# Order of the row scatters, the routing steps and the residual steps on the queues of an attention and mixture-of-experts kernel

## The chip, the cores and the metric

The kernel runs on one core of one Trainium2 chip, in one launch. The metric is device time in microseconds. Three timed runs of the kernel before gave 1774.93, 1779.41 and 1780.96 us, so its time is the median, 1779.41 us. The profile comes from a separate execution in which the hardware profiler recorded every instruction.

A core has five engines with a queue of instructions each: PE (matrix products; its weight loads are listed apart as PEld), DVE (elementwise work on vectors), ACT (activations and copies), POOL (a general engine that here also issues the indirect transfers) and SP (which here only issues transfers). Each queue runs in order. Transfers are issued from POOL's and SP's queues and are carried out by 16 DMA engines.

## The reference, cut to what matters

The input is four sequences (batches) of 512 tokens of width 512. A first attention over the context adds to x; then comes a transformer block with causal attention and a mixture of experts. The change concerns the mixture and how its rows are laid out.

```python
x1 = x + xattn(layernorm(x), ctx)             # context attention, one per batch
hid = layernorm(x1)
h = rmsnorm(hid, ln1_w)                        # causal attention, 16 heads of 128
q, k, v = (heads(h @ w) for w in (wq, wk, wv))
ao = softmax(causal(q @ k.T / sqrt(128))) @ v
x2 = hid + merge(ao) @ wo
t = rmsnorm(x2, ln2_w).reshape(-1, 512)        # 2048 rows
probs = softmax(t @ gate_w.T)                  # 16 experts
topv, topi = top_k(probs, 6)
topv = topv / sum(topv)
cw = zeros(2048, 16).at[row, topi].add(topv)
routed = sum over e of cw[:, e] * ((silu(t @ eg_w[e].T) * (t @ eu_w[e].T)) @ ed_w[e].T)
shared = (silu(t @ sg_w.T) * (t @ su_w.T)) @ sd_w.T
out = x1 + x2 + routed + shared
```

An expert has 352 hidden features, the shared expert 704.

## The kernel before, in words

**Precision.** Operands of PE are split into a high and a low half-precision part, and each product is three matmuls (high by high, high by low, low by high). The helper that issues them gives nearly every matmul one of three source lines: L83, L86 and L87. The helper that splits a result (a copy on ACT and a subtraction on DVE or POOL) gives L73, L74, L77 and L78. So matmuls are told apart by the names of their tiles.

**Attention.** The outer loop runs over 64 heads `n`, in the order of `path`: batches 0 and 1 in turn by groups of two heads, then batches 2 and 3 likewise, so that a batch ends well before its partner's last groups. In each step PE does `queries` of head n (tile `qk`), every second step `values` (`v`), then, if a group is done, `project` (`wo`, four matmul groups over two banks, added into `x2` at L681), then `scores` of head n (`sc`, with the softmax on DVE and ACT and a transposing transfer of the result), and `attend` of head n-1 (`av`, evicted to `ao`). A generator, `step`, feeds in the context attention of the next batches (tiles `xm`, `hd`, `x_d`, `r`).

**Routing.** When the eighth group of a batch is projected, `route1` runs at once: sums of squares on ACT (`rsq`), then `rsqrt` (an addition on DVE and a power on POOL, L104, tile `rrs`), then for each of four row tiles the normalised rows `h2` (L494), their split into `h2p` and a transposing transfer by SP's queue into `h2T`. It also appends four entries to `rest`. `agenda` then calls `route2` at step n+2 and `route3` at step n+3. `route2` makes the gate's logits on PE (tile `lg`, L520, 64 small matmuls), the softmax, the top 6 and one-hot codes on DVE, and running sums over the experts and the product of probabilities on POOL (L559 to L562). `route3` counts rows per expert on PE (`rk`) and POOL, gives every row and choice a slot (L590, L591 and others), and appends 24 scatters to the list `scat`: four row tiles by six choices.

**Scatters, marks and residual steps.** A scatter (L463) is an indirect transfer from POOL's queue that writes the 128 rows of one `h2p` tile to their slots in `xs_d`, the experts' input in DRAM. Scatters are declared independent of each other, since their slots differ. `pace(src)` copies one element to `mark` on POOL (L455); it must wait for `src`, a result of the stage that runs then, and so holds what stands behind it on POOL's queue. `rest_step` loads a tile of the saved first residual (`x1t`, L506), adds `x2` (L509) and stores the sum to `r_d`. The list `scats` holds the marks and scatters made so far.

**Order of the queues.** The kernel is written in program order and a scheduler, which simulates the engines' times, decides the order in each queue. What must stay in order without data behind it is given by `after(ins, first)`, which adds a dependence for the order only. In the kernel before each mark and each scatter is placed behind the last entry of `scats`.

**Shared expert.** `gate_up` runs in six blocks `ic` for a batch (tiles `sg` and `su`, with SiLU at L710 and the product at L713 into `hs`); `shared_down` makes four row tiles `sy` and adds them into an accumulator `acc` at L735, which `residual(b)` loads from `r_d` over SP's queue (L689). Batch 0's shared expert runs at the end of the attention, then batch 1's (`up(1)`), with batch 3's `route2` and `route3` among its blocks, then batch 2's (`up(2)`). `drip(n, src)` is a mark and then up to n scatters. `rows_in` loads the first expert's rows from `xs_d`, transposed, into `xT`, again over SP's queue.

**Experts.** Sixteen experts follow in the order of their row counts (`g` and `u`, then `y`, stored to `y_d`), batch 3's shared expert comes last, and 96 indirect gathers (L1149) collect the results.

Of the kernel before, what the change touches and what calls it, by code (L numbers as in the profile page):

```python
# [10 lines left out]
F32 = mybir.dt.float32  # L11
# [3 lines left out]
ALU = mybir.AluOpType  # L15
AX = mybir.AxisListType

P = 128
B, S, D = 4, 512, 512
# [36 lines left out]
def xattn_moe_block_kernel(ctx: ExitStack, tc: tile.TileContext, x, xT, ctxT, wqkx, bqk, ln1, ln2,  # L56
# [36 lines left out]
    def after(ins, first):  # L93
        tc.add_manual_dep(ins.ins, first.ins.name,
                          mybir.DependencyInfo(mybir.DependencyClass.NoSync, mybir.DependencyReason.DATA),
                          reason="order on the queue")
# [4 lines left out]
    def rsqrt(o, v, eps):  # L101
        n = o.shape[1]
        nc.vector.tensor_scalar(o, v, eps, None, ALU.add)
        nc.gpsimd.tensor_tensor(o, o, mhalf[:, :n], ALU.pow)  # L104

    ident = const.tile([P, P], F32, name="ident")
    make_identity(nc, ident)
# [345 lines left out]

    def pace(src):
        ins = nc.gpsimd.tensor_copy(mark, src)  # L455
        if scats:
            after(ins, scats[-1])
        scats.append(ins)

    def scatter(n):  # L460
        while scat and n:
            tt, k = scat.pop(0)
            ins = nc.gpsimd.indirect_dma_start(  # L463
                out=xs_d, out_offset=bass.IndirectOffsetOnAxis(ap=slotu[:, tt, k:k + 1], axis=0),
                in_=h2ps[tt], in_offset=None)
            tc.declare_no_dep(ins.ins, group="scat", reason="the slots differ")
            tc.add_to_no_dep_group("scat", ins.ins)
            if scats:
                after(ins, scats[-1])
            scats.append(ins)  # L470
            n -= 1

# [8 lines left out]
    def route1(b, x2):  # L481
        ms = bsm.tile([P, NT], F32, name="rms")
        for t in range(NT):
            sq = xp.tile([P, D], F16, tag="h2", name="rsq", bufs=1)
            nc.scalar.activation(sq, x2[:, t, :], AF.Square, scale=1.0 / math.sqrt(D),
                                 accum_out=ms[:, t:t + 1])
        rr = bsm.tile([P, NT], F32, name="rrs")
        rsqrt(rr, ms, 1e-6)
        h2T[b] = hpool.tile([P, 2 * C, S], F16, tag="hT", name=f"h2T{b}")
        for t in range(NT):  # L490
            tt = b * NT + t
            tl = slice(t * P, (t + 1) * P)
            h2 = xp.tile([P, D], F32, tag="h2", name="h2", bufs=1)
            nc.vector.scalar_tensor_tensor(h2, x2[:, t, :], rr[:, t:t + 1], ln2b, ALU.mult, ALU.mult)  # L494
            h2p = h2ps[tt] = rp.tile([P, 2 * D], F16, tag="h2p", name="h2p", bufs=4)
            split1(h2p[:, :D], h2p[:, D:], h2, nc.vector if b == B - 1 else nc.gpsimd)
            zz["flip"] = flip(h2T[b][:, :, tl], h2p)
            rest.append((b, t, x2))
# [3 lines left out]
    def rest_step():  # L502
        if rest:
            b, t, x2 = rest.pop(0)
            x1t = xp.tile([P, D], F32, tag="x1t", name="x1t", bufs=1)
            ins = nc.gpsimd.dma_start(x1t, x1_d[b][:, t, :])  # L506
            if scats:
                after(ins, scats[-1])
            nc.gpsimd.tensor_tensor(x1t, x1t, x2[:, t, :], ALU.add)  # L509
            nc.gpsimd.dma_start(r_d[b][:, t, :], x1t)  # L510

# [53 lines left out]
    def route3(b):  # L565
        nonlocal macc
        oh, mm, cs, pr = zz[b]
        bs = slice(b * NT, (b + 1) * NT)
        rk = bank("s", f"rk{b}")
        for t in range(NT):  # L570
            o = rk[:, t * E:(t + 1) * E]
            nc.tensor.matmul(o, su, mm[:, t, :], start=True, stop=False)
            nc.tensor.matmul(o, onesm, macc, start=False, stop=True)
            m2 = const.tile([P, E], F16, tag="macc", name=f"macc{b}_{t}", bufs=3)
            nc.gpsimd.tensor_tensor(m2, macc, mm[:, t, :], ALU.add)
            macc = m2
        rb = rp.tile([P, NT, E], F32, name="rb", bufs=1)
        nc.vector.tensor_tensor(rb, rk[:, :NT * E].rearrange("p (t e) -> p t e", e=E),
                                ebase.unsqueeze(1).to_broadcast([P, NT, E]), ALU.add)
        o4 = oh.rearrange("p (t k) e -> p t k e", k=K)  # L580
        w4 = rp.tile([P, NT * K, E], F32, name="w4", bufs=1)
        for t in range(NT):
            nc.vector.tensor_tensor(o4[:, t], cs[:, t, :].unsqueeze(1).to_broadcast([P, K, E]),
                                    kp1.unsqueeze(2).to_broadcast([P, K, E]), ALU.is_equal)
        for dst, val in ((slot, rb), (cw, pr)):
            for t in range(NT):
                nc.gpsimd.tensor_tensor(w4[:, t * K:(t + 1) * K, :], o4[:, t],
                                        val[:, t, :].unsqueeze(1).to_broadcast([P, K, E]), ALU.mult)
            nc.vector.tensor_reduce(dst[:, bs, :].rearrange("p t k -> p (t k)"), w4, AX.X, ALU.add)
        nc.gpsimd.tensor_tensor(w4, oh, ioe.unsqueeze(1).to_broadcast([P, NT * K, E]), ALU.mult)  # L590
        nc.vector.tensor_reduce(tid[:, bs, :].rearrange("p t k -> p (t k)"), w4, AX.X, ALU.add)  # L591
        nc.vector.tensor_copy(slotu[:, bs, :], slot[:, bs, :])
        for t in range(NT):
            for k in range(K):
                scat.append((b * NT + t, k))
# [160 lines left out]
    for n in range(NH + LAG + 1):  # L756
        if n < NH:
            b, h = heads[n]
            if b not in opened:
                opened.add(b)  # L760
                step(b, 99)
                if b == B - 1:
                    shared_pool()
            parts = [queries(b, h)]
            if h % HG == 0:
                parts.append(values(b, h // HG))
            if n == 0:
                parts.reverse()
                for p in parts:
                    next(p)  # L770
            for p in parts:
                for _ in p:
                    pass
        m = n - LAG
        if n >= NH:
            for ic in range(3 * (n - NH), 3 * (n - NH) + 3):
                hs0 = next(early)
                if scat:
                    pace(hs0[ic // 3][0:1, ic % 3, 0, 0:1])
                    scatter(-(-len(scat) // (6 - ic)))  # L780
        if ready:
            b, g = ready.pop()
            project(b, g)
            left[b] -= 1
            if not left[b]:
                route1(b, x2s[b])
                agenda[n + 2] = agenda[n + 3] = b
                if stop == "B":
                    nc.sync.dma_start(out[b].rearrange("(t p) d -> p t d", p=P), x2s[b])
        if n < NH:  # L790
            scores(*heads[n])
        if 0 <= m < NH:
            b, h = heads[m]
            attend(b, h)
            if h % HG == HG - 1:
                ready.append((b, h // HG))
        if n in agenda and n < NH:
            b = agenda[n]
            if n + 1 in agenda:
                route2(b)  # L800
            else:
                route3(b)
        if m > 0 and (rest or scat):
            pace(aos[heads[m - 1][0], heads[m - 1][1] // HG][0:1, heads[m - 1][1] % HG, 1, 0:1])
        rest_step()
        if scat and n < NH:
            scatter(-(-len(scat) // (min(x for x in ends if x > n) - n + (4 if n > NH - 3 else 0))))
        shared_weights()
        if H // 2 <= n < H // 2 + E:
            pad_rows(n - H // 2)  # L810
        if n < 6:
            step(1, 2)
        else:
            for _, j in zip(range(2 - n % 2), bring):
                step(j)
# [12 lines left out]
    def up(b):  # L828
        return gate_up(b, lambda: st2.tile([P, 6 * S], F16, name="hs"), lambda: st2.tile([P, S], F32, name="sgt"))

    def drip(n, src):
        if scat:
            pace(src)
            scatter(n)

    ups = enumerate(up(1))
    _, hs = next(ups)
    route2(B - 1)
    for _, hs in zip(range(3), ups):
        hs = hs[1]  # L840
    route3(B - 1)

    cps = bank("s", "cnt")
# [22 lines left out]
            nc.vector.tensor_tensor(o, o, t, ALU.add)  # L866
        return o

    for _, hs in ups:
        pass  # L870
    drip(1, hs[1][0:1, 2, 0, 0:1])
    shared_down(1, hs, tick=lambda src: drip(2, src))
    residual(2)
    after(zz["exp"], zz["silu", 1, 1])
# [100 lines left out]
    seat(0)  # L975
    nxt = ranked_weights(0)
    for ic, hs in enumerate(up(2)):
        drip(3, hs[ic // 3][0:1, ic % 3, 0, 0:1])
        if ic == 4:
            rows_in(0, 0)  # L980
            rows_in(0, 1)
    shared_down(2, hs)
# [291 lines left out]
```

## Time and profile before

| | |
|---|---|
| median of three timed runs | 1779.41 us |
| the profiled execution's own time | 1810.57 us |
| its span, first to last instruction | 1808.8 us |
| mean granted clock of PE in it | 0.98 |
| DVE / ACT / POOL busy | 62% / 46% / 26% of the span |
| scatters L463 | 96, of 1009 ns mean, 96.8 us together |
| gathers L1149 | 96, of 1129 ns mean, 108.4 us together |
| transfers | 296.24 MB, mean 164 GB/s |

The profiled execution took 31.16 us more than the median of the timed runs, and 1.8 us of its time lie outside its span. Places in the text are given in microseconds from the start of the span. In a line of the timeline the first number is the start, the second the duration of the instruction or run of like instructions, then come engine, source line, operation, the tiles written and read, and in brackets the idle time of the engine just before it with what ended it. "issue" there means that the engine waited for nothing that the profile shows, "remote" for something that is not on this core or not known. In a list of waits the numbers are the total, how often, and the longest.

### The profile page before, as it was taken

What the parts mean: (1) busy time and instruction counts of PE and PEld (TensorE: products, weight loads), DVE (VectorE), ACT (ScalarE), POOL (GpSimd) and SP (SyncE); (2) the same over time, 40 slices, a digit from 0 to 9 for tenths busy, and PEclk for the clock granted to TensorE, in tenths of its full rate; (3) what the DMA queues carried; (4) which work ended last, traced back from release to release, by engine and by line L of the source; (5) the groups of instructions that cost most, each with busy time, mean ns of one, the idle gap of its engine ahead of it and who ended that gap; (6) DMA issues with size and microseconds to landing.
All of it is one profiled execution on the core that took longest, in us unless ns stands there. A gap on an engine that the chain in (4) does not pass through costs nothing. (4 is left out here: it accounts for less than half of the span.)

```text
span 1808.8 us, 27686 instructions
## 1 busy us (share of the span) xinstructions
PE 1731.3 (96%) x9919; PEld 937.2 (52%) x9919; DVE 1113.3 (62%) x2766; ACT 830.0 (46%) x1711; POOL 469.0 (26%) x580
## 2 busy tenths in 40 slices
PE   8799999999998999999999899999999999999997
PEld 3454545555554555556555344355555555555453
DVE  7786777777784677776667543744443444356655
ACT  5554645455543545554445322334444444444321
POOL 5323111130246243121113534400000000036453
PEclk9899999999998999999999899999999999999999
DMA  7876767465586777555547533575555545589866
GB/s 239 206 171 177 212 149 184 109 190 115 126 186 189 151 174 184 123 122 111 113 101 151 149 95 117 203 192 149 147 148 175 146 145 144 174 218 267 209 191 200
DMA packets 392724, 296.24 MB, mean 164 GB/s; under 512 B 334880, under 2 KB 335136, under 8 KB 391808
## 3 DMA queue, kind: packets, MB, share of 16 engines
q1 hardware_dynamic: 359456, 180.32, 42.7%
q0 software_dynamic: 33120, 114.06, 20.2%
q8 instruction: 80, 1.31, 0.3%
q14 instruction: 68, 0.56, 0.1%
HBM read 124.81 MB, written 88.94 MB: 118 GB/s over the span
## 5 line engine op out<-in xcount | busy, mean ns | idle before, releaser
L1149 POOL DMA_INDIRECT yg<-y_d,yrc x96 | 108.4, 1129 | 512.8 <-DVE hf L1052 426.3
L649 ACT ACTIVATE pe<-pe,bnm 128x128 f32<-128x128 f32 (+3 forms) x256 | 142.3, 557 | 162.3 <-DVE bnm L647 154.7
L83 PE MATMUL qk<-hT,wqk 128*128 128x512 f16 (+1 forms) x520 | 196.7, 378 | 6.7 <-DMA hT<-hh 6.7
L86 PE MATMUL qk<-hT,wqk 128*128 128x512 f16 (+1 forms) x520 | 196.6, 378 | 0.0
L87 PE MATMUL qk<-hT,wqk 128*128 128x512 f16 (+1 forms) x520 | 196.5, 378 | 0.0
L74 DVE SCALAR_TENSOR_TENSOR pn<-pe,brc,pn 128x128 f16<-128x128 f32 (+3 forms) x256 | 146.5, 582 | 22.6 <-ACT pn L73 17.4
L647 DVE CUSTOM_DVE_ANT_0 pe<-sc,causal 128x128 f32<-128x128 f32 (+3 forms) x256 | 117.2, 486 | 66.9 <-PE sc L644 58.0
L73 ACT ACTIVATE pn<-pe,brc 128x128 f16<-128x128 f32 (+3 forms) x256 | 133.7, 553 | 27.8 <-ACT pe L649 16.4
L86 PE MATMUL v<-wv,hT 128*128 128x256 f16 x512 | 141.1, 276 | 2.5 <-issue 2.5
L87 PE MATMUL v<-wv,hT 128*128 128x256 f16 x512 | 141.1, 276 | 2.5 <-issue 2.5
L83 PE MATMUL v<-wv,hT 128*128 128x256 f16 x512 | 141.1, 276 | 0.8 <-DMA hT<-hh 0.8
L83 PE MATMUL g<-xT,wt 128*128 128x384 f16 (+2 forms) x384 | 127.8, 333 | 2.3 <-DMA xT<-xs_d 2.3
L86 PE MATMUL g<-xT,wt 128*128 128x384 f16 (+2 forms) x384 | 127.8, 333 | 0.0
L87 PE MATMUL g<-xT,wt 128*128 128x384 f16 (+2 forms) x384 | 127.8, 333 | 0.0
L681 DVE SCALAR_TENSOR_TENSOR x<-wo,x 128x512 f32<-128x512 f32 x128 | 87.5, 687 | 38.8 <-PE wo L87 38.5
L1038 ACT ACTIVATE hT_e<-hf 128x384 f16<-128x384 f32 (+3 forms) x96 | 51.0, 531 | 128.9 <-DVE hf L1052 113.7
L83 PE MATMUL y<-dt,hT_e 128*128 128x512 f16 (+1 forms) x288 | 110.0, 382 | 0.0
L86 PE MATMUL y<-dt,hT_e 128*128 128x512 f16 (+1 forms) x288 | 109.4, 380 | 0.0
L87 PE MATMUL y<-dt,hT_e 128*128 128x512 f16 (+1 forms) x288 | 109.4, 380 | 0.0
L73 ACT ACTIVATE qkt<-qk 128x512 f16<-128x512 f32 x128 | 74.9, 588 | 71.5 <-PE qk L87 70.8
L463 POOL DMA_INDIRECT xs_d<-h2p,slotu x96 | 96.8, 1009 | 26.8 <-issue 25.6
L1052 DVE SCALAR_TENSOR_TENSOR hf<-u,sg 128x384 f32<-128x384 f32 (+2 forms) x64 | 36.5, 570 | 105.1 <-PE u L87 101.5
(323 smaller groups left out, 4094.2 us busy)
## 6 DMA issues: line engine op xcount, KB each, us to landing
y_d<-yt SPq DMA_DIRECT2D x96, 256.0 KB
est<-in_ew_dram SPq DMA_DIRECT2D x32, 704.0 KB
est<-in_ed_dram SPq DMA_DIRECT2D x16, 768.0 KB
wqk<-wqk_d POOLq DMA_DIRECT2D x20, 512.0 KB
wqk_st<-in_wqk_dram SPq DMA_DIRECT2D x16, 512.0 KB
wqk_d<-wqk POOLq DMA_DIRECT2D x15, 512.0 KB
xs_d<-causal POOLq DMA_DIRECT2D x16, 384.0 KB
wv<-wv_d POOLq DMA_DIRECT2D x10, 512.0 KB
```

The source lines that it names most:

```text
L73: return (nc.scalar.activation(hi, src, AF.Copy, scale=scale), nc.vector.scalar_tensor_tensor(lo, src, scale, hi, ALU.mult, ALU.subtract))
L74: nc.vector.scalar_tensor_tensor(lo, src, scale, hi, ALU.mult, ALU.subtract))
L83: ins = nc.tensor.matmul(o, lh, rh, start=start and j == 0, stop=False)
L86: nc.tensor.matmul(o, lh, rl, start=False, stop=False)
L87: ins = nc.tensor.matmul(o, ll, rh, start=False, stop=stop and j == n - 1)
L463: ins = nc.gpsimd.indirect_dma_start(out=xs_d, out_offset=bass.IndirectOffsetOnAxis(ap=slotu[:, tt, k:k + 1], axis=0), in_=h2ps[tt], in_of ...
L647: nc.vector.tensor_tensor_reduce(pe, ps[:, :w], causal[:, S - w:], -1.0, 3e38, ALU.add, ALU.min, nm)
L649: nc.scalar.activation(pe, pe, AF.Exp, bias=nm, scale=-1.0, accum_out=sm)
L681: nc.vector.scalar_tensor_tensor(x2[:, t, :], ps, 1.0 / (VS * WS), x2[:, t, :], ALU.mult, ALU.add)
L1038: nc.scalar.activation(hT[:R, ic, :w], hf, AF.Copy)
L1052: nc.vector.scalar_tensor_tensor(hf, pu, GS * PSC, sg, ALU.mult, ALU.mult)
L1149: nc.gpsimd.indirect_dma_start(out=yg, out_offset=None, in_=src, in_offset=bass.IndirectOffsetOnAxis(ap=idx[:, tt, k:k + 1], axis=0))
```

## The change

- `rsqrt` returns its power instruction, and `route1` keeps it in `zz["rrs"]`.
- `pace` puts the mark behind that instruction and behind every entry of `scats`, and then leaves only itself in the list. `scatter` puts each scatter behind the first entry, which now is the last mark. `rest_step` still goes behind the last entry.
- In the attention loop the agenda's block (`route2` or `route3`) stands before `scores` and `attend` of the step, not behind them.
- For the last batch `h2` comes from a pool with two buffers (tag `pe3`) in place of one with a single buffer.
- In the tail two blocks of `up(1)` stand before `route2(B - 1)` and two before `route3(B - 1)`, where it was one and three. The drips are two scatters at block 4 and two at block 5, where it was one after block 5; in `up(2)` they are four per block, where it was three; and `rows_in` comes after block 3, where it was block 4.

```diff
@@ -101,7 +101,7 @@
     def rsqrt(o, v, eps):
         n = o.shape[1]
         nc.vector.tensor_scalar(o, v, eps, None, ALU.add)
-        nc.gpsimd.tensor_tensor(o, o, mhalf[:, :n], ALU.pow)
+        return nc.gpsimd.tensor_tensor(o, o, mhalf[:, :n], ALU.pow)
 
     ident = const.tile([P, P], F32, name="ident")
     make_identity(nc, ident)
@@ -453,9 +453,11 @@
 
     def pace(src):
         ins = nc.gpsimd.tensor_copy(mark, src)
-        if scats:
-            after(ins, scats[-1])
-        scats.append(ins)
+        if "rrs" in zz:
+            after(ins, zz["rrs"])
+        for s in scats:
+            after(ins, s)
+        scats[:] = [ins]
 
     def scatter(n):
         while scat and n:
@@ -466,7 +468,7 @@
             tc.declare_no_dep(ins.ins, group="scat", reason="the slots differ")
             tc.add_to_no_dep_group("scat", ins.ins)
             if scats:
-                after(ins, scats[-1])
+                after(ins, scats[0])
             scats.append(ins)
             n -= 1
 
@@ -485,12 +487,13 @@
             nc.scalar.activation(sq, x2[:, t, :], AF.Square, scale=1.0 / math.sqrt(D),
                                  accum_out=ms[:, t:t + 1])
         rr = bsm.tile([P, NT], F32, name="rrs")
-        rsqrt(rr, ms, 1e-6)
+        zz["rrs"] = rsqrt(rr, ms, 1e-6)
         h2T[b] = hpool.tile([P, 2 * C, S], F16, tag="hT", name=f"h2T{b}")
         for t in range(NT):
             tt = b * NT + t
             tl = slice(t * P, (t + 1) * P)
-            h2 = xp.tile([P, D], F32, tag="h2", name="h2", bufs=1)
+            h2 = (he.tile([P, D], F32, tag="pe3", name="h2") if b == B - 1 else
+                  xp.tile([P, D], F32, tag="h2", name="h2", bufs=1))
             nc.vector.scalar_tensor_tensor(h2, x2[:, t, :], rr[:, t:t + 1], ln2b, ALU.mult, ALU.mult)
             h2p = h2ps[tt] = rp.tile([P, 2 * D], F16, tag="h2p", name="h2p", bufs=4)
             split1(h2p[:, :D], h2p[:, D:], h2, nc.vector if b == B - 1 else nc.gpsimd)
@@ -504,8 +507,8 @@
             b, t, x2 = rest.pop(0)
             x1t = xp.tile([P, D], F32, tag="x1t", name="x1t", bufs=1)
             ins = nc.gpsimd.dma_start(x1t, x1_d[b][:, t, :])
-            if scats:
-                after(ins, scats[-1])
+            for s in scats[-1:]:
+                after(ins, s)
             nc.gpsimd.tensor_tensor(x1t, x1t, x2[:, t, :], ALU.add)
             nc.gpsimd.dma_start(r_d[b][:, t, :], x1t)
 
@@ -787,6 +790,12 @@
                 agenda[n + 2] = agenda[n + 3] = b
                 if stop == "B":
                     nc.sync.dma_start(out[b].rearrange("(t p) d -> p t d", p=P), x2s[b])
+        if n in agenda and n < NH:
+            b = agenda[n]
+            if n + 1 in agenda:
+                route2(b)
+            else:
+                route3(b)
         if n < NH:
             scores(*heads[n])
         if 0 <= m < NH:
@@ -794,12 +803,6 @@
             attend(b, h)
             if h % HG == HG - 1:
                 ready.append((b, h // HG))
-        if n in agenda and n < NH:
-            b = agenda[n]
-            if n + 1 in agenda:
-                route2(b)
-            else:
-                route3(b)
         if m > 0 and (rest or scat):
             pace(aos[heads[m - 1][0], heads[m - 1][1] // HG][0:1, heads[m - 1][1] % HG, 1, 0:1])
         rest_step()
@@ -833,11 +836,12 @@
             pace(src)
             scatter(n)
 
-    ups = enumerate(up(1))
-    _, hs = next(ups)
+    ups = up(1)
+    for _, hs in zip(range(2), ups):
+        pass
     route2(B - 1)
-    for _, hs in zip(range(3), ups):
-        hs = hs[1]
+    for _, hs in zip(range(2), ups):
+        pass
     route3(B - 1)
 
     cps = bank("s", "cnt")
@@ -866,9 +870,8 @@
             nc.vector.tensor_tensor(o, o, t, ALU.add)
         return o
 
-    for _, hs in ups:
-        pass
-    drip(1, hs[1][0:1, 2, 0, 0:1])
+    for ic, hs in zip((4, 5), ups):
+        drip(ic // 2, hs[1][0:1, ic - 3, 0, 0:1])
     shared_down(1, hs, tick=lambda src: drip(2, src))
     residual(2)
     after(zz["exp"], zz["silu", 1, 1])
@@ -975,8 +978,8 @@
     seat(0)
     nxt = ranked_weights(0)
     for ic, hs in enumerate(up(2)):
-        drip(3, hs[ic // 3][0:1, ic % 3, 0, 0:1])
-        if ic == 4:
+        drip(4, hs[ic // 3][0:1, ic % 3, 0, 0:1])
+        if ic == 3:
             rows_in(0, 0)
             rows_in(0, 1)
     shared_down(2, hs)
```

## The prediction

> **What bounds the kernel now.** I read the page first, for the engine that fills the span, then PE's own waits, then tables of busy time over the stretches where PE was idle, and last the timeline of POOL there, since the change moves POOL's instructions.
>
> ```profile
> span 1808.8 us, 27686 instructions
> PE 1731.3 (96%) x9919; PEld 937.2 (52%) x9919; DVE 1113.3 (62%) x2766; ACT 830.0 (46%) x1711; POOL 469.0 (26%) x580
> ...
> PEclk9899999999998999999999899999999999999999
> ```
>
> PE is the bound: 1731.3 us busy at a mean granted clock of 0.980 is about 1697 us of full-speed work, so 112 us of the span are idle time or slow clock. Only those 112 us are to be had. Where they lie near the change:
>
> ```profile
> 546.00:560.40 14.40, 14.38 (x90) 8.37 (x89) 8.88 (x27) 4.98 (x13) 11.35 (x13) 1.00 0.73 192
> 560.40:579.80 19.40, 12.42 (x47) 5.21 (x47) 3.43 (x9) 2.74 (x7) 13.52 (x16) 0.65 0.73 244
> 1011.20:1023.70 12.50, 12.50 (x64) 5.95 (x62) 6.41 (x21) 7.69 (x16) 9.89 (x11) 1.00 0.65 205
> 1023.70:1043.20 19.50, 11.78 (x32) 3.78 (x31) 3.83 (x6) 2.45 (x4) 12.08 (x14) 0.65 0.46 158
> ```
>
> The columns are length, then busy time of PE, PEld, DVE, ACT, POOL, then granted clock, DMA share and GB/s. In the second and fourth rows PE, DVE and ACT all nearly stop and only POOL works, at a mean clock of 0.65. What POOL does there is one back-to-back train of row scatters (L463):
>
> ```profile
> 1011.22 1.08 POOL L463 DMA_INDIRECT xs_d<-h2p,slotu  x1 [0.17 <-DVE bnm L647]
> ...
> 1023.95 0.38 PE L86 MATMUL sg<-h2T,shw 128*128 128x512 f16 x1 [0.24 <-issue]
> ...
> 1031.74 0.60 ACT L73 ACTIVATE ao<-av 128x512 f16<-128x512 f32 x1 [10.84 <-remote]
> ...
> 1033.88 0.96 POOL L463 DMA_INDIRECT xs_d<-h2p,slotu  x1 [0.30 <-issue]
> ```
>
> A scatter goes out every 1.27 us from 1011.2 to 1034.8. PE's gaps are put down to "issue", ACT's to nothing on the core. In 1023 to 1034 the two instruction queues moved no packet, while each neighbouring stretch has one. I read this as engines waiting for their next instructions behind the train. Batch 0 has the same (train from 546.1 to 577.0, stall from 560.4), batch 3 a smaller one. The other waits that the change touches:
>
> ```profile
> PE lg L520 <- DMA h2T<-h2p: 4.9, 1, 4.9
> PE g L83 <- DMA xT<-xs_d: 2.3, 1, 2.3
> ...
> ACT sgt L710 <- remote: 22.6, 1, 22.6
> DVE tid L591 <- POOL w L590: 6.4, 1, 6.4
> DVE h L494 <- POOL rrs L104: 4.8, 1, 4.8
> ```
>
> **The change part by part.** Sums are against the profiled execution, 1810.57 us (span 1808.8 plus 1.8 around it). The median of the three timed runs is 1779.41, 31.2 us less; I come back to that.
>
> 1. *Scatters ordered behind the last mark (L455).* The chain through `scats[-1]` was lost between scatters, since they are declared independent; only the first after a mark was held. Now all are, and the queue as scheduled shows the groups. Batch 0 was 5, a mark, 16, a mark and 1 (22 in the train up to 577.0), then 1 and 1 later; it becomes 5, 5, 5, 5, 4, one group per head (about 14 us, of which five scatters take 6.4). Batch 2 was 4, a mark and 14 (the train above), then six single ones; it becomes 4, 4, 3, 3, 3, 3, 2, 2. Batch 3 was 13, 2 and nine single ones; it becomes 2, 2, 2, 2, 2, 2, 4, 4, 4. Batch 1 had no long train: 5 scatters, with 0.5 us of PE gap after them.
>  Batch 0: between 560.4 and 579.8 PE did 20 `v` matmuls (0.113 us each from the 48 that took 5.4), 9 `sc` (1.15), 12 `av` (1.8) and 4 `xm` (0.86): 6.1 us of work in 19.4, so 13.3 lost. Batch 2: 5 `sg` and 24 `su` at 0.215 (12 take 2.58): 6.2 in 19.5, lost 13.3. Batch 3: 12 `su` from 1137.96 took 6.0 instead of 2.75, and the next table's matmul (L958) waited 0.8: lost 4.0. Together 30.6.
>  No instruction is added, one mark (0.2 to 1.8 us on POOL) goes. What now queues behind a waiting mark on POOL: weight loads (L413), the `x_d`, `r`, `hd` steps of the next batch, and L590, for which DVE waits at L591. For batch 0, L590 comes after ten scatters, some 3 us after DVE reaches L591 by my count; PE has `v` and `qk` work of 5 us in between, so I cost it at nothing; without that cover, 3 us.
>  Does spreading leave a rest of the stall? In batch 2 the groups of 3 take 3.8 us out of each 5.2 us block of `sg` and `su`. Bounds 0 and 13.3; nearest row is batch 1's 0.5 us for five; I take 3.
>
> 2. [...] The row above says three stalls of 30.6 us. [...] I side with the row, since PE, ACT and DVE stop together in each of the three trains and go on as each ends.
>
> 3. *Norm root first (L104, pow 1.05 us).* For batch 3 it waited from 1069.9 to 1074.1 behind a residual add; `lg` then waited 4.85 us for the last transpose, and 32 `lg` with 12 `sg` took 5.5 us instead of 3.5 at the low clock: lost 6.9. Now the root runs at 1070, h2 has two buffers, and `lg` stands two `sg`/`su` blocks later (about 1088). The transposes should land by 1085. All 6.9 goes.
>  What is late next: the four residual steps (load, add, store) now all follow the root. Each takes about 8 us with its waits (1061.0 to 1069.3 and on), so POOL reaches the routing's L562 at about 1101.4 and the second running count at 1103.5, while PE's `rk` comes at about 1101.8: a new wait of 2 us (bounds 0 and 6.9).
>
> 4. *Rows fetched earlier.* The last scatter was issued at 1169.4, at the fifth `up(2)` block; `g` waited 2.3 us for the rows, and 12 `g` took 3.5 instead of 2.1. With 4 per mark the last goes out after the third block, about 20 us sooner; 3.7 goes. But on SP's queue the accumulator load of batch 2 (L689, issued at 1164.62) now stands behind three row transposes of 3.2 us each. Scatters end near 1148, land by 1154 (5.8 us as before), so the load is issued near 1164 and lands near 1168, while that stage's `sy` start at about 1153. Three banks hold three of four `sy`; the fourth wants its bank at 1165 and gets it near 1169.5: 4.4 plus 1.5 of slow clock, 6 (bounds 0 and 7).
>
> 5. *Routing half a head sooner, batches 0 to 2.* `lg` now stands among the four `wo` groups instead of behind `sc`. The 64 `lg` (1.8 us) are the same work. For batch 0 the last `h2p` goes from 506.8 to about 508.2 on POOL, because two x1t steps now come between, and its transpose lands near 514; PE reaches those `lg` near 516.6. Batch 2 gives 981 against 983. So no wait, by 2 us. But `qk` no longer fills the gaps while DVE empties the two `wo` banks (evictions at 515.9 to 521.6 before). I take 1.5 us for each of three (bounds: below nothing, as `av` waited 1.39 us for its transpose at 533 and may not now, and 6.9, the measured price at batch 3).
>
> Sum: 30.6 + 6.9 + 3.7 = 41.2 off; 3 + 2 + 6 + 4.5 = 15.5 on; 25.7 net. Profiled it would be 1785. The timed runs lose less: 1779.41 less 1.8 and 1697 leaves 81 of the profile's 112 us, a factor of 0.72. I scale: 18.5 us, so 1779.4 - 18.5 = 1761.
>
> **The rivals.**
> - *The stalls belong to the traced execution.* [...] Then 10.6 comes off and 12.5 goes on: 1.9 slower, about 1781. Against it: the stalls follow the trains and not the number of recorded instructions; in 546.0 to 560.4, inside the same train, PE is busy 14.38 of 14.40 us with 219 instructions of PE, PEld, DVE and ACT recorded, and it stops only once the train has run that long.
> - *Slower: every group stalls a little.* If the fetch is held up while any scatters are in flight, the 22 groups each cost something instead of three trains. At 2 us each it is 44 on, 30.6 and 10.6 off, 12.5 on: 15 worse, scaled 11, 1790. It decides from about 1.3 us a group (22 x 1.3 = 28.7). Batch 1 speaks against it with 0.5 us for five scatters.
> - *`lg` waits three times.* At 6.9 each instead of 1.5 the net falls to 9.5, scaled 7: 1772. It turns to slower only from a wait of about 8 us each, where my margins are 2.
> - *The groups do not come about.* The scheduled queue shows them, so I give it nothing.
>
> **How the numbers follow.** The measurement tells about 0.3% (5 us) from no change. The main case has 0.55 (1761, its own range 1750 to 1772), three waits at `lg` 0.07 (1772, faster), traced only 0.17 (1781, no change), every group stalling and the worse end of `lg` 0.21 (1790, slower). Low end: the 25.7 unscaled gives 1753.7, and without the rest of 3 and half the accumulator's wait 1748; 1746 leaves 0.05 below. The upper end of 1788 takes in the traced-only case and leaves about 0.14 above.
>
> **What would show it.** Right: no stretch near batch 0's or batch 2's scatters with PE, DVE and ACT idle together and a clock of 0.65; groups of at most five L463; no wait of `lg` for h2T; `g` without its 2.3 us. The new wait should stand at DVE L735 of batch 2 behind the accumulator load. Wrong: gaps put down to "issue" after each group, or `lg` waiting for h2T at batches 0 to 2, or a span shorter by 25 us with timed runs unchanged.

## The result: 0.8% slower, and the stalls that it was to remove were not there

Eleven timed runs of the changed kernel have a median of 1789.63 us (1783.6 to 1797.95), eleven of the kernel before 1773.24 us (1768.08 to 1780.96). The ratio is 1.0078, with a 95% interval of 1.0055 to 1.0100: about 14 us slower, where the prediction had 18 us faster. Yet the profile of the changed kernel is shorter than the one that the prediction was read from:

```profile
span 1782.4 us, 27673 instructions
...
PE 1715.3 (96%) x9919; PEld 934.0 (52%) x9919; DVE 1115.1 (63%) x2766; ACT 829.6 (47%) x1711; POOL 473.5 (27%) x579
...
PEclk9999999999999999999999998999999999999999
```

Its own time, 1784.62 us, lies within the range of its timed runs. The profiled execution of before, 1810.57 us, does not: it is 30 us above the slowest of the eleven runs. So the first thing to test was that profile. (Of one kernel below, S T, the profiled execution took 1800.41 us against a median of 1784.03, so of it only the tail is read.) PE's waits in the changed kernel (total, how often, longest):

```profile
PE rk L575 <- DVE mm L557: 11.5, 1, 11.5
PE av L83 <- DMA pt<-pn: 9.3, 6, 2.9
...
PE wo L83 <- DVE x L684: 4.3, 5, 1.7
...
PE av L83 <- DVE i L543: 2.3, 1, 2.3
...
PE g L83 <- DMA xT<-xs_d: 0.7, 1, 0.7
...
PE lg L523 <- DMA h2T<-h2p: 0.3, 1, 0.3
```

The waits of `lg` for `h2T` (4.9 us) and of `g` for its rows (2.3 us) are all but gone (0.3 and 0.7), as forecast. In their place stands one wait of `rk` of 11.5 us, and during the routing of batches 0 and 2 PE waits for DVE: for `x`, the eviction of `wo`, and for `i`, the top 6. (Lines after the edits are three higher than in the kernel before.)

### The profile page after: what moved, and what is told of

It reads as the page before. It is cut to its first block, busy times and chain, and to the rows that moved or that the text cites. A ratio compares the mean times of both kernels' runs of the same rounds, so it can differ in the third digit from the quotient of the medians.

```text
span 1782.4 us, 27673 instructions
## 1 busy us (share of the span) xinstructions
PE 1715.3 (96%) x9919; PEld 934.0 (52%) x9919; DVE 1115.1 (63%) x2766; ACT 829.6 (47%) x1711; POOL 473.5 (27%) x579
## 4 chain that ended last, share of the span: by engine, by line
PE 55%; DMA 4%; issue 3%; POOL 2%; DVE 1%; ACT 0%; POOLq 0%; SPq 0%; ACTq 0%
PE g L86 3%; PE g L83 3%; PE g L87 3%; PE y L83 3%; PE y L86 3%; PE y L87 3%; PE u L83 2%; PE u L87 2%; PE u L86 2%; PE qk L87 2%; PE qk L86 2%; PE qk L83 2%; PE wo L83 1%; PE wo L87 1%; PE wo L86 1%
## 5 line engine op out<-in xcount | busy, mean ns | idle before, releaser
L83 PE MATMUL v<-wv,hT 128*128 128x256 f16 x512 | 139.6, 273 | 0.9 <-DMA hT<-hh 0.9
L87 PE MATMUL v<-wv,hT 128*128 128x256 f16 x512 | 139.6, 273 | 0.0
L86 PE MATMUL v<-wv,hT 128*128 128x256 f16 x512 | 139.6, 273 | 0.0
L465 POOL DMA_INDIRECT xs_d<-h2p,slotu x96 | 101.2, 1054 | 29.4 <-issue 27.7
L83 PE MATMUL wo<-wo,ao 128*128 128x512 f16 x256 | 97.6, 381 | 5.5 <-DVE x L684 4.3
```

Of the source, the lines that this page charges most:

```text
L83: ins = nc.tensor.matmul(o, lh, rh, start=start and j == 0, stop=False)
L86: nc.tensor.matmul(o, lh, rl, start=False, stop=False)
L87: ins = nc.tensor.matmul(o, ll, rh, start=False, stop=stop and j == n - 1)
L465: ins = nc.gpsimd.indirect_dma_start(out=xs_d, out_offset=bass.IndirectOffsetOnAxis(ap=slotu[:, tt, k:k + 1], axis=0), in_=h2ps[tt], in_of ...
```

## The experiments

The parts are named S (marks and scatters ordered behind the last mark), L (routing sooner in the attention loop), R (marks behind the norm root, `h2` in two buffers) and T (the tail: two blocks ahead of route2, drips, rows one block sooner).

**The kernel before, profiled again.** No edit.

> The kernel before, unchanged, in a second profiled execution. If the three stalls behind the scatter trains (13.3 us near 560, 13.3 us near 1023, 4.0 us near 1138) belong to the kernel, they stand here again in the same places and the span is near 1808 us. If they belonged to the one execution that the prediction was read from, the span is near 1772 us, as the timed runs have it, and PE has no gaps of 0.65 clock behind the trains.

Its time was 1776.42 us, its span 1774.7. Four stretches of it, cut at the first instruction of each batch's norm root on DVE (L103, tile `rrs`) and at the first matmul `g` of the experts, and after them batch 2's train. A stretch is called by the batch whose root opens it; the last is the tail. Columns: length, then busy time of PE, PEld, DVE, ACT and POOL, granted clock, DMA share, GB/s.

```profile
484.30:608.90 124.60, 120.52 (x780) 69.21 (x778) 90.30 (x277) 60.15 (x146) 63.37 (x89) 0.99 0.84 191
608.90:940.00 331.10, 329.83 (x2089) 192.78 (x2088) 233.15 (x676) 169.91 (x407) 77.17 (x118) 1.00 0.60 132
940.00:1036.20 96.20, 96.20 (x601) 51.97 (x600) 59.49 (x172) 46.03 (x100) 50.98 (x77) 1.00 0.57 148
1036.20:1146.50 110.30, 100.28 (x510) 43.94 (x510) 62.18 (x185) 29.26 (x43) 46.82 (x65) 0.96 0.50 159
...
990.70:1014.40 23.70, 23.70 (x122) 11.44 (x120) 11.58 (x30) 11.84 (x23) 18.78 (x21) 1.00 0.66 216
```

The last row holds the train of 18 scatters that the prediction charged with 13.3 us: PE is busy for all of its 23.70 us at full clock. The third row, the whole of batch 2's routing, has no idle time at all, and from 480 us on no wait of PE put down to "issue" is over 0.9 us. So the three stalls do not belong to every execution of this order. What brought them about, no run shows; none of the later profiles of either order has them. In the changed kernel the same stretches are:

```profile
480.10:609.90 129.80, 122.51 (x794) 70.96 (x793) 91.71 (x276) 60.19 (x146) 63.97 (x89) 0.99 0.77 184
609.90:943.30 333.40, 328.61 (x2075) 191.57 (x2074) 234.06 (x675) 169.50 (x406) 77.66 (x118) 1.00 0.59 131
943.30:1048.60 105.30, 100.39 (x604) 53.09 (x603) 61.05 (x173) 45.85 (x100) 52.33 (x75) 0.97 0.52 135
1048.60:1157.40 108.80, 95.85 (x490) 42.32 (x488) 57.56 (x181) 29.25 (x43) 50.57 (x69) 0.94 0.50 157
```

So the changed kernel loses 5.2, 2.3 and 9.1 us in the three stretches of the loop and gains 1.5 in the tail: 15.1 us, near the 14 us of the timed runs. (Ahead of the first stretch and in the experts, which the change leaves as they were, this profile of the changed kernel is 4.2 and 3.2 us shorter than that of before.) All experiments are read in this way:

| kernel | ratio to before (95%) | batch 0 | batch 1 | batch 2 | tail |
|---|---|---|---|---|---|
| before, second profile | 1 | 124.6 | 331.1 | 96.2 | 110.3 |
| changed (S L R T) | 1.0078 (1.0055 to 1.0100) | 129.8 | 333.4 | 105.3 | 108.8 |
| S | 1.0031 (1.0010 to 1.0053) | 140.3 | 333.9 | 96.2 | 104.1 |
| S again | 1.0033 (1.0012 to 1.0053) | 131.4 | 332.9 | 96.2 | 104.4 |
| S in sixes | 0.9961 (0.9942 to 0.9980) | 125.0 | 331.7 | 96.2 | 104.1 |
| L | 1.0117 (1.0089 to 1.0145) | 134.6 | 334.3 | 100.6 | 109.1 |
| L, route2 only | 1.0097 (1.0058 to 1.0135) | 138.7 | 335.0 | 98.2 | 107.7 |
| L, route3 only | 1.0088 (1.0053 to 1.0124) | 136.8 | 336.0 | 98.3 | 108.3 |
| R | 1.0056 (1.0030 to 1.0081) | 126.0 | 333.2 | 97.2 | 109.8 |
| T | 0.9943 (0.9919 to 0.9966) | 130.2 | 331.4 | 96.2 | 98.1 |
| T again | 0.9932 (0.9911 to 0.9952) | 123.6 | 330.7 | 96.2 | 97.0 |
| T, R for batch 3 only | 0.9995 (0.9976 to 1.0014) | 124.0 | 333.3 | 96.2 | 104.9 |
| S T | 1.0036 (1.0018 to 1.0054) | not read | | | 104.4 |
| S in sixes, T | 0.9996 (0.9972 to 1.0021) | 124.0 | 332.9 | 96.2 | 104.6 |
| S R T | 1.0107 (1.0064 to 1.0149) | 135.3 | 333.2 | 97.3 | 105.4 |
| S L T, h2 in two buffers | 1.0020 (1.0000 to 1.0040) | 135.5 | 330.4 | 100.4 | 101.8 |
| changed, four buffers | 1.0047 (1.0026 to 1.0067) | 131.1 | 334.1 | 105.3 | 101.2 |
| changed, in sixes | 1.0002 (0.9979 to 1.0024) | 133.2 | 332.6 | 104.4 | 108.9 |
| S in sixes, T, four buffers | 0.9863 (0.9828 to 0.9899) | 129.2 | 331.1 | 96.2 | 98.3 |

A ratio comes from many runs, a stretch from one profiled execution; T and T again, the same kernel, show 130.2 and 123.6 for batch 0, so a difference of 6 us there is not read, and neither is the 5.2 us of the changed kernel. Batch 2's column is the steadiest: 96.2 wherever L and R are both absent from the loop, 97.2 and 97.3 with R, 98.2 to 100.6 with L, 104.4 to 105.3 with both.

Each ratio is to runs of before on the same chip, but not all kernels ran on one. The medians of before lie between 1773.24 and 1777.63 us, except on the chip of the last two rows, where it is 1793.91. At the same granted clock of 0.989 the runs of before average 1791 us there and 1775 to 1777 on four other chips. What slows before there is not known, and it was not profiled there. The two ratios may owe as much to this as to their edits, so they are not compared with those of the other rows.

**S alone, twice.** The edits of `pace` and `scatter`, without the norm root.

```diff
-        if scats:
-            after(ins, scats[-1])
-        scats.append(ins)
+        for s in scats:
+            after(ins, s)
+        scats[:] = [ins]
...
-                after(ins, scats[-1])
+                after(ins, scats[0])
```

> The kernel before with the new ordering of marks and scatters alone (pace and scatter; no wait for the norm root, routing and tail as before). If the train stalls are there in the timed runs, this alone takes 18 to 25 us off (about 1750). If they belonged to one execution, it is within 5 us of before (1773), or slower by a few us where weight loads of POOL's queue stand behind more waiting marks.

> The scatter ordering alone once more, beside the groups of six on the same chip: 0.3% slower than before, with waits of av for pt near 604 and of qk for wqk near 559, if those waits belong to the order of the queue; without them if they belonged to one execution.

0.3% slower both times: without the trains the timed runs got no faster, so on these two chips they had no 30 us of stalls to give. In the first profile PE stopped at batch 0's `av`, and the transfers issued there from 583 to 606 took (count, size, median us from issue to landing):

```profile
604.35 0.58 PE L83 MATMUL av<-pt,vt 128*128 128x512 f16 x1 [11.56 <-DMA pt<-pn]
...
wqk<-wqk_d POOLq DMA_DIRECT2D x1, 512.0 KB, 9.5
wv<-wv_d POOLq DMA_DIRECT2D x1, 512.0 KB, 12.3
pt<-pn SPq DMA_TRANSPOSE x6, 11.3
xs_d<-h2p,slotu POOLq DMA_INDIRECT x4, 11.0
```

In the second profile of before, from 586 to 606:

```profile
wv<-wv_d POOLq DMA_DIRECT2D x1, 512.0 KB, 3.9
wqk<-wqk_d POOLq DMA_DIRECT2D x1, 512.0 KB, 8.2
...
pt<-pn SPq DMA_TRANSPOSE x6, 2.4
xs_d<-h2p,slotu POOLq DMA_INDIRECT x1, 5.5
```

The spread order puts a fifth group, of four scatters, between the loads of `wqk` and `wv`. They land together with the transposes of the softmax, which take 11.3 us in place of 2.4, and PE waits. Earlier, near 559, `qk` waited 4.2 us for `wqk`, where before has no such wait. In the repeat, with the same loads and scatters at the same places, `av` waited 2.7 us for `pt` and `qk` 2.7 us for `wqk`. The size of the collision thus differs from execution to execution, and part of it needs no new order: T alone, which leaves batch 0's order as it was, had a wait of `av` for `pt` of 5.6 us at 602.2, and the second profile of before one of 2.7 at 557.9.

**S in groups of six for batch 0**, so that the fifth group is not there:

```diff
-            scatter(-(-len(scat) // (min(x for x in ends if x > n) - n + (4 if n > NH - 3 else 0))))
+            scatter(6 if scat[0][0] < NT else -(-len(scat) // (min(x for x in ends if x > n) - n + (4 if n > NH - 3 else 0))))
```

> The scatter ordering alone, with batch 0's scatters in four groups of six, so that the fifth group is gone that went out beside a row weight load and a value weight load near 587 to 592 (where PE then waited 11.6 us for the transposes of the softmax). If the collision of that group with those loads and transposes is what the scatter ordering costs, av's wait near 604 is under 3 us, the stretch from batch 0's norm root to batch 1's falls from 140 us to 125 to 130, and the kernel is 5 to 10 us faster than the ordering in groups of five. If any spreading costs, by the marks that weight loads stand behind, it stays as slow, with waits of qk for wqk.

On the same chip 0.39% faster than before, where S was 0.33% slower: about 13 us from the number of groups alone (medians of 1769.7 and 1782.1 us). The two stretches of batch 0, S again and S in sixes:

```profile
486.40:617.80 131.40, 123.22 (x780) 69.91 (x778) 91.50 (x277) 60.29 (x145) 63.31 (x89) 0.96 0.80 182
```

```profile
482.60:607.60 125.00, 118.80 (x779) 68.52 (x777) 90.34 (x275) 60.12 (x145) 63.38 (x88) 1.00 0.81 191
```

S in sixes is no shorter in the loop than before, only no longer. What it gains lies in the tail (104.1 against 110.3), and S in groups of five has that, too (104.1 and 104.4). The longest wait of `av` after 500 us is 2.5 us, and no wait of `qk` for `wqk` is left. That the 13 us are the fifth group's collision is argued, not shown: the two stretches differ by 6.4 us, no more than T's two profiles do, and `av` waits hardly less (2.5 us against 2.7).

**L alone, and its halves.** The agenda's block ahead of `scores`; then with `route2` or `route3` alone moved there.

> The kernel before with routing half a head sooner alone. By the prediction's step 5 it costs 4.5 us (1.5 for each of batches 0 to 2). If the routing's DVE chain (top 6, one-hot) standing ahead of the softmax of the same head holds PE, it costs 5 to 12 us in all, with waits of wo and av on DVE at the three routings.

> The kernel before with route2 alone ahead of scores and attend, route3 where it was. If what costs is the logits' place among the wo groups, or the long DVE chain of softmax and top 6 ahead of the head's own softmax, nearly all of loop_only's 20 us is here. If it is route3 and the scatters that start sooner, this is within 5 us of before.

> The kernel before with route3 alone ahead of scores and attend, route2 where it was. If route2's place is what costs, this is within 5 us of before. If route3's slots and the sooner scatters cost, it is 10 to 20 us slower.

L is the costliest part, 1.17% or some 21 us, more than either expectation, and each half alone costs most of it (17 and 16 us): neither is the innocent one that the two tests looked for. In L's profile PE waited for an eviction behind the routing and then for transposes, which took a median of 11.0 us among those issued from 515 to 536 (5.0 in the second profile of before):

```profile
504.56 0.38 PE L83 MATMUL wo<-wo,ao 128*128 128x512 f16 x1 [2.29 <-DVE x L681]
...
534.71 0.58 PE L83 MATMUL av<-pt,vt 128*128 128x512 f16 x1 [7.54 <-DMA pt<-pn]
...
wqk<-wqk_d POOLq DMA_DIRECT2D x1, 512.0 KB, 9.3
wv<-wv_d POOLq DMA_DIRECT2D x1, 512.0 KB, 12.1
pt<-pn SPq DMA_TRANSPOSE x4, 11.0
```

No scatter is in flight there; the first goes out at 540.1. But routing's work now stands ahead of the load of `wqk` on POOL's queue: it leaves 38.3 us after the root in place of 33.5, and 2.8 us ahead of the load of `wv` in place of 7.9.

With L alone batch 0's stretch grew by 10.0 us, batch 1's by 3.2 and batch 2's by 4.4. That the transposes are late by collision with the two weight loads is argued from these latencies; no run here takes those loads away. With `route3` alone moved, the load of `wqk` leaves at 33.5 as before, and `av` waits later, 5.0 us at 594.8; what costs there is not settled.

**R alone, and S R T.**

> The kernel before with the last batch's norm root ahead of the marks, and h2 in two buffers, alone. By the prediction's step 3 it takes up to 6.9 us off. By the rival that the residual steps now end later and hold the tile hs, and behind it the softmax of the gate on DVE, it gives 5 to 11 us back: between same and 5 us slower.

> The changed kernel with routing put back behind scores and attend in the attention loop; all else as changed. If the earlier routing is what costs (it cost 20 us alone) and the parts add up, this is 1776 + 5 for the scatters - 10 for the tail, near 1771 plus whatever the norm root costs. If the norm root ahead of the residual steps is a cost of its own (rk waited 11.5 us in the changed kernel's profile), it stays 6 to 11 us above that, near 1780.

R costs 0.56%, twice what was allowed for. S R T, the changed kernel without L, was expected near 1771 to 1780 and came out at 1.0107: taking L away brought nothing, though its profile has batch 2's 8 us back (97.3 against 105.3). The parts do not add up. S R T shows in batch 0 what S shows (`av` waits 9.3 us for `pt`, `qk` 2.3 us for `wqk`) and in the tail what R shows (`rk` waits 8.1 us).

**T alone, twice.**

> The kernel before with the tail's changes alone: two blocks of up(1) ahead of route2, drips of two, four scatters a block in up(2), rows one block sooner. By the prediction's step 4 rows fetched earlier take 3.7 us off and the accumulator wait puts up to 6 on; route2 one block later should take the 4.9 us wait of lg off: between 4 us faster and 3 us slower. If what costs the time in the changed kernel is in the tail itself, it is over 5 us slower.

> The tail's changes alone once more, on another chip: 0.6% faster than before if the gain of 12 us that its profile shows between batch 3's norm root and the first expert's matmul (98 us in place of 110) is the kernel's; within 0.3% if it was that chip's or that execution's.

T is 0.6 to 0.7% faster on both chips, 10 to 11 us where at most 4 were expected, and the tail's stretch falls from 110.3 to 98.1 and 97.0 us. This is what the changed kernel has, too, and loses again. Where it loses it, its timeline shows (start, duration, engine, line, operation, tiles, and in brackets the wait and what ended it):

```profile
1053.40 1.60 POOL L512 TENSOR_TENSOR x1t<-x1t,x 128x512 f32<-128x512 f32 x1 [1.35 <-DMA x1t<-x_d]
...
1064.29 0.54 POOL L509 DMA_DIRECT2D x1t<-x_d  x1 [8.18 <-DMA r_d<-x1t]
...
1084.77 1.26 POOL L512 TENSOR_TENSOR x1t<-x1t,x 128x512 f32<-128x512 f32 x1 [2.97 <-DMA x1t<-x_d]
1086.06 1.15 ACT L77 ACTIVATE hs<-sgt 128x512 f16<-128x512 f32 x2 [16.20 <-POOL x1t L512]
...
1086.72 0.69 DVE L78 TENSOR_TENSOR hs<-sgt,hs 128x512 f16<-128x512 f32 x1 [16.61 <-ACT hs L77]
...
1091.30 0.17 PE L575 MATMUL rk<-mm,su 128*128 128x16 f16 x1 [11.48 <-DVE mm L557]
```

No data goes from `x1t` to `hs`; `hs` comes from a pool that is opened on memory of the pools closed before it, so I read the wait as one for memory whose last reader is the addition: a buffer of `x1t` or of `x2`. The four residual steps share one buffer and follow each other, the last addition ends at 1086.03, `hs` waits for it, DVE's part of `hs` stands ahead of the rest of the gate's softmax in DVE's queue, and `rk` waits for that.

**Four buffers for the last batch's residual loads**, in the changed kernel:

```diff
-            x1t = xp.tile([P, D], F32, tag="x1t", name="x1t", bufs=1)
+            x1t = (hq.tile([P, D], F32, tag=f"qk{t % 2}", name="x1t") if b == B - 1 else
+                   xp.tile([P, D], F32, tag="x1t", name="x1t", bufs=1))
```

> The changed kernel with four buffers in place of one for the last batch's four residual loads (taken from a pool that the attention has left). If the tile hs, and behind it DVE's gate softmax and rk, wait for the last of the four serial residual steps (11.5 us at rk in the changed kernel's profile), the steps now overlap, the last add ends some 10 us sooner, rk's wait falls under 3 us, and the kernel gains about 9 us (1789 to 1780). If rk waits for something else, the wait stays and the time is the changed kernel's.

The last addition now ends at 1066.9, 13 us after the batch's norm root began on DVE in place of 37.5; no `hs` waits for it any more, and no wait of `rk` is left; `lg` waits 4.6 and 1.7 us for `h2T` again. The tail falls from 108.8 to 101.2 us, and the ratio is 1.0047 in place of 1.0078 (the intervals overlap), a gain of some 5 us where 9 were expected.

```profile
1053.90:1155.10 101.20, 94.93 (x491) 42.30 (x490) 62.72 (x180) 29.26 (x43) 49.11 (x69) 0.97 0.60 170
```

**Pairs and remainders.** T with R for the last batch only, S with T, and the changed kernel without the marks' wait for the root:

> The kernel before with the tail's changes and the marks' wait for the norm root for the last batch only, so that batches 0 to 2 keep their order. If that wait costs in the tail, rk waits 6 to 11 us in the profile, the tail's gain of 10 us is gone, and the time is near before (1776). If the cost of the norm root alone (10 us) lay in the order of batches 0 to 2, this keeps the tail's gain (1766).

> The kernel before with the scatter ordering and the tail's changes, without the norm root and the sooner routing. If the parts add up, 5 us slower and 10 us faster than before: 1771. If the spread scatters gain nothing but collide with the transposes of the softmax (waits of av for pt near 600), it is slower than the tail's changes alone (1766). If the stalls behind the trains were a cost of the timed runs too, it is faster than those, under 1760.

> The changed kernel without the marks' wait for the norm root (h2 stays in two buffers). If that wait is what undoes the tail's gain (rk behind the residual steps), this is about 10 us faster than the changed kernel, near 1780, and its rk does not wait. If the loss lies in the sooner routing and the spread scatters alone, it is within 4 us of the changed kernel.

The first lost T's gain while batches 0 to 2 kept their lengths, so R's price in the tail is shown. The second came to 1784.03 us, not to the 1771 of parts that add up: with S, too, `hs` waits longer for the last residual addition than with T alone (13.5 us against 8.7 and 9.3), presumably as the marks hold the residual steps. Over the profiles `rk` waits more than 1 us only where `hs` waits long: none where `hs` waits up to 9.3 us (T, T again), 3.8 us where it waits 11.9 (S L T), 6.0 at 13.5 (S T), 7.9 at 12.6 (T with R for batch 3), 11.5 at 16.2 (changed). The third came to 1.0020, 1780.49 us, near what was expected, though its `rk` still waits.

**The last two.**

> The tail's changes with the scatter ordering in groups of six for batch 0. If the fifth group's collision was all that the ordering cost, this is as fast as the tail's changes alone (0.6% faster than before); if spreading brings anything of its own, it is faster still.

> The tail's changes, the scatter ordering with groups of six for batch 0, and four buffers for the last batch's residual loads. Groups of six alone were 0.4% faster than before and the tail's changes 0.6 to 0.7%, but together no faster, with rk waiting 6 us behind the tile hs, which waited 15 us for the last residual add. If that wait is what ate the gain, it is gone here, the stretch from batch 3's norm root to the first expert falls from 105 to 98 us, and the kernel is 0.8 to 1.1% faster than before (1758 to 1763). If not, it stays at the time of before.

> The changed kernel with batch 0's scatters in groups of six and nothing else. If the collision of the fifth group is a good part of its loss, batch 0's stretch falls from 130 to about 125 us and the kernel gains 5 to 10 us, to within 0.4% of before. If its loss lies in the sooner routing and in rk's wait, it gains under 4 us.

S in sixes with T was no faster than before: `hs` waited 15.0 us and `rk` 6.2. With four buffers besides no wait of `rk` is left, and its tail is back at T's length:

```profile
1042.60:1141.00 98.40, 95.50 (x494) 42.62 (x494) 60.73 (x180) 29.15 (x44) 47.78 (x67) 0.98 0.56 173
```

`hs` still waits 3.3 us for the last addition, though `x1t` lies in another pool now, which speaks for the buffers of `x2`. On that chip before took 1793.91 us and this version 1767.3, 1.37% less. But T alone took 1765.88 and 1766.43 us on two other chips, so this version is not shown to be faster than T. The changed kernel in sixes came to 1794.2 us, the time of before on that chip (1.0002), where the changed kernel took 1789.63 elsewhere. Its profile shows no gain: batch 0's stretch is no shorter (133.2 against 129.8), `rk` still waits 11.4 us, and the changed kernel's own profile has no collision at the fifth group, where its two loads are 10.7 us apart in place of S's 6.6. So whether groups of six help the changed kernel stays open.

## Why the prediction was wrong, by its steps

1. **The step that failed** is part 1, 30.6 us for three stalls behind the trains, and with it "I side with the row" of part 2. The row was true of one execution; the second profile of the same order has none of these stalls (23.70 of 23.70 us busy), and taking the trains away with S alone cost 0.3% where 18 to 25 us would have come off. The sign was there: the profile stood 31.2 us above the median of the timed runs, nearly the 30.6 us of the three stalls. The missing instruction packets were no sign: the second profile has none from 1018.2 to 1043.4 either, and PE did not stop up to 1036.2, where the table's stretch ends (96.20 of 96.20 us busy), while batch 0's stall, 560.4 to 579.8 in the first profile, has one. The rival that the stalls belong to the traced execution was right for the chips on which this was tried (whether it holds for the one on which before reached 1812.07 us is open). Scaling the net by 0.72 spread the excess over all terms, where nearly all of it sat in one.
2. **A rest of 3 us after spreading** was asked of the wrong engine. S did not cost by groups that stop PE's instructions: in its first profile PE's longest wait put down to "issue" is 2.1 us. Its profiles show waits of `av` for transposes (11.6 us, 2.7 in the repeat) and of `qk` for a weight load (4.2 and 2.7), and a tail 6 us shorter: 0.3%, or 5 to 6 us net. The weight loads behind marks were named in the step, but only the wait at L591 was given a price, and it was put at nothing; the transposes were not named.
3. **Norm root first.** The 6.9 us came off, but not by the root alone: T, without it, brings the waits of `lg` from 5.2 to 1.2 us by the later place of `lg`, while R alone leaves 2.0 and costs 0.56%. The new wait at `rk` was forecast at 2 us (bounds 0 and 6.9) by POOL's queue at L562 and measured 11.5: it came by a buffer, through ACT and DVE. The four residual steps took 36.1 us where about 8 each was forecast; of the 11.5 us some 6.2 went by until the last addition ended, and 5.3 in what `hs` had held back on ACT and DVE.
4. **Rows fetched earlier.** `g`'s wait fell from 2.3 to 0.7 us. The six microseconds charged to the accumulator of batch 2 did not come: no profile with T shows PE waiting for it over 0.9 us. T's gain of 12 to 13 us in the tail is the sum of the two terms named, 6.9 and 3.7, and a little more.
5. **Routing half a head sooner** was mis-sized: 4.5 us forecast, 21 us alone. The bound of 6.9 a batch was meant for `lg` waiting; `lg` never waited more than 0.3 us in the changed kernel. What waited was what stands behind the routing on DVE, and the transposes. The rival of three waiting `lg` had the right place and the wrong instruction. (It would have made the kernel slower from a wait of about 10 us each by its own sum, not 8.)

The rival that landed nearest in time, 1790 by stalls at every group, is wrong in its mechanism: from 480 us on, the changed kernel has no wait of PE put down to "issue" over 1.9 us.

## What to carry to other kernels

Compare a profiled execution's own time with the spread of the timed runs before anything is read from it; where it lies outside, profile again, since a stall that only one execution has can carry most of the sum: here 30.6 of the 41.2 us that were to come off. Where a transfer is moved, a scatter or a weight load, look at what it now lands beside, and for the transposes that a matmul waits for: here `av` waited 11.6 us for them where four scatters went out between two weight loads, and 7.5 us where two such loads stood 2.8 us apart. Compare ratios only where the kernel before is as fast as elsewhere. And where an order is made later, follow the buffer as well as the queue: who takes over the memory of what now ends last.

## What the runs showed of the hardware

In the stretch of the collision the transposes by DMA were drawn out most, 4.7 times, against 2.0 for the scatters and 3.2 for the load of `wv`: with S the median from issue to landing was 11.3 us in place of 2.4 when four scatters (11.0 us in place of 5.5) went out between two loads of 512 KB (the second of which, `wv`, took 12.3 us in place of 3.9). With L it was 11.0 beside two such loads 2.8 us apart and no scatter. It is no fixed price: in the repeat of S, from 585 to 612, the transposes took 6.8 us and the scatters 6.0. A lower granted clock went with the idle time: S's batch 0 has 17.2 us of idle PE against 4.1 and is 15.7 us longer, as PE's busy time grew, too, from 120.5 to 123.1 us for about the same number of matmuls, at a mean granted clock of 0.94 in place of 0.99.
